# Two 32-column transposes in place of one 64-column transpose in a conditioned recurrent layer

## The chip, the cores and the metric

The kernel runs on one core of a Trainium2 chip. The core has five engines with instruction queues of their own: TensorE (PE in the profile; its weight loads are shown as PEld), VectorE (DVE), ScalarE (ACT), GpSimd (POOL) and SyncE (SP, which here only issues DMAs). The metric is the device time of one execution in microseconds.

## What is computed

```python
xT = jnp.swapaxes(x, 0, 1)
def step(h, x_t):
    fused = jax.nn.sigmoid(jnp.concatenate([x_t, h], axis=-1) @ w_W + w_b)
    hidden_state, output_state = jnp.split(fused, 2, axis=-1)
    memory_state = x_t @ wx_W + wx_b + hidden_state * (h @ wh_W + wh_b)
    h_new = output_state * h + (1.0 - output_state) * jnp.tanh(memory_state)
    return (h_new, h_new)
_, hs = jax.lax.scan(step, h0, xT)
return x + jnp.swapaxes(hs, 0, 1)
```

`x` is 8 x 512 x 512 (batch, time, features), the state `h` is 8 x 512, everything in float32. The loop of 512 steps is serial: each needs the `h` that the one before made. In the names of the kernel, `r` is `hidden_state`, `z` is `output_state`, and **hh** is `h @ wh_W + wh_b`.

## The kernel before

**Layout.** The 512 features of the state lie as 128 partitions x 4 chunks (k = 0 to 3) x 8 batches. Chunks 0 and 1 are half A (`hf = 0` in the code), chunks 2 and 3 are half B (`hf = 1`). One step of the loop over `i` (512 of them, written out, no loop on the chip) belongs to a group `g` of four steps; the buffers `md0`, `md1` and the PSUM banks alternate with `g % 2`.

**TensorE in a step** (L219, the helper `mm`). The order is A0 A1 A2 A3 D0 D1 D2 D3 H2 H3, the digit being the chunk of `h` that is the stationary operand: bank A receives 256 columns for chunks 0 and 1 and 192 for 2 and 3, bank D 128, bank H 64. Behind them come, in each step, some products of the input with its weights for a chunk of time 17 steps ahead (tiles `xp`); they depend on nothing in the step. A0 to A3 need the new state of their chunk, so A2 of the next step needs the new state of chunk 2, the first chunk of half B.

**VectorE in a step.** The order of its queue is the order in which the code is written (the schedule is manual). From the first wait on bank A:

1. `turn_r` L577 `tr<-A` transposes r of half A; `turn_h(0)` L592 `md1A<-A`; `turn_z` L577 `tz<-A` and the small memset `settle(0)` L600.
2. `memory(0, 0)` and `memory(0, 1)`: scans L565 `m<-md0A,md1A`, each followed on ScalarE by a tanh (L285 `hT<-m`).
3. `turn_part` L636 `md1B<-A`; `turn_r_b` L577 `tr<-D`, whose results ScalarE turns into `md0B` with one sigmoid for each chunk (L285 `md0B<-tr`), and into `sz` with one more.
4. `update(0, 0)` (L565 `hT<-hd0A,hT`, new state of chunk 0); **`turn_h(1)` L592 `md1B<-H`**, which transposes hh of half B, 128x64 in PSUM bank H, into slot 1 of `md1B` for both chunks of the half; `update(0, 1)`; **`settle(1)` L600**, a memset of one column that waits for `h_done[1]`, the completion of that transpose.
5. `memory(1, 0)` and `memory(1, 1)`: scans L565 `m<-md0B,md1B` of chunk 2 and chunk 3, each followed by its tanh.
6. `turn_sz` L629 `hd0B<-sz`: two transposes of 128x32, then a memset L632 that waits for the first of the two; `update(1, 0)` and `update(1, 1)` (L565 `hT<-hd0B,hT`), the new state of chunks 2 and 3.
7. Sums of the input products (L431), turns of the input parts (L319) and two memsets (L710) fill the time until bank A of the next step is complete.

**Waits.** An instruction here waits for a semaphore in its own queue, and all behind it wait too. VectorE also waits for itself: a scan that reads what a VectorE instruction shortly before it has written needs a wait for that write. One instruction carries one wait; a second one costs an instruction of the queue's own (EVENT_SEMAPHORE, engine DVEq in the trace). The memsets L600 and L632 carry such waits in place of it. ScalarE's tanh needs its scan, `update` needs its tanh and the transposed `z`.

**Names of the change.** `md1[hf][g % 2]` is seen as partition x 32 rows x 2 chunks x slots; in memory the chunk is the outer one. `raw["h"][1]` is `ps["H"]`, 64 columns, 32 for each chunk. `h_done` is set by `turn_h` and read by `settle`.

Of the kernel before, what the change touches and what calls it, by code (L numbers as in the profile page):

```python
# [76 lines left out]
def tile_cond_rnn_residual(  # L77
# [38 lines left out]
    nc = tc.nc  # L116
# [54 lines left out]
    def pair(n, name, rows, slots):  # L171

        return const.tile([P, 2, rows, slots], F32, name=name).rearrange("p c n s -> p n c s")
# [3 lines left out]
    NH = 2 * GS  # L177
# [4 lines left out]
    md1 = [[pair(n, f"md1{n}{i}", 32, m) for i in range(2)] for n, m in (("A", 2), ("B", 3))]  # L182
# [340 lines left out]
    pool_done = {}  # L523
    for i in range(T):
        g, s = divmod(i, GS)
        c, t = divmod(i, TC)
# [46 lines left out]
        raw = {"h": (pa[:, :HU], ps["H"]), "z": (pa[:, HU : 2 * HU],), "r": (pa[:, 2 * HU :], ps["D"][:, HU:])}  # L573
# [6 lines left out]
        h_done = [None, None]  # L580
# [8 lines left out]
            )  # L589

        def turn_h(hf):
            inst = nc.vector.transpose(  # L592
                md1[hf][g % 2][:, :, :, hf].rearrange("p n c -> p c n"), raw["h"][hf]
            ).ins
            h_done[hf] = inst
            if hf == 0 and i + 1 - NH in pool_done:
                tc.add_manual_dep(inst, pool_done[i + 1 - NH].name, SYNC)

        def settle(hf):
# [53 lines left out]

        turn_r()
        turn_h(0)
        turn_z()
        memory(0, 0)
# [6 lines left out]
        sz = turn_r_b()  # L664
        update(0, 0)
        turn_h(1)
        update(0, 1)
        settle(1)
# [146 lines left out]
```

## Time and profile before

| | |
|---|---|
| median of 3 runs | 1628.59 us (1627.81 to 1628.85) |
| span of the profiled execution | 1625.9 us |
| PE busy | 1616.3 us, 99% of the span |
| DVE busy | 1411.1 us, 87% |
| ACT busy | 1023.8 us, 63% |
| POOL busy | 539.1 us, 33% |
| granted TensorE clock | 1.000 |

The span runs from the first to the last instruction of the profiled execution; the median of the runs lies 2.7 us above it, which is what surrounds the instructions (the profiled execution has no other time of its own). Starts in a timeline are printed to 10 ns. A matmul's start is recorded and its end modelled. In a row of groups, the numbers after the bar are total busy time, mean duration in ns, and the idle time of the engine before the group with what ended it.

### The profile page before, as it was taken

Reading aid. Unit: us, or ns where it says so; the run is one execution under the profiler, and the core shown is the slowest. Engines: PE = TensorE matmul, PEld = TensorE weight load, DVE = VectorE, ACT = ScalarE, POOL = GpSimd, SP = SyncE. Lnnn points to the kernel's source line nnn. Section 1 sums busy time; section 2 is a strip of 40 time slices with the busy share of each in tenths; the row PEclk is TensorE's granted clock in tenths of the full one; section 3 lists DMA queues with packets and bytes.
Section 4 is the critical chain, followed back from the end, with each engine's and each line's share of the span. In section 5 each row is a group of like instructions: output and inputs, shape, how many; then the busy total and the mean of one; then the engine's idle time right before and its main releaser. Section 6 shows DMA issues by size and latency. Waiting matters only on the chain.

```text
span 1625.9 us, 120027 instructions
## 1 busy us (share of the span) xinstructions
PE 1616.3 (99%) x49211; PEld 1308.3 (80%) x49211; DVE 1411.1 (87%) x11757; ACT 1023.8 (63%) x6033; POOL 539.1 (33%) x1443
## 2 busy tenths in 40 slices
PE   9999999999999999999999999999999999999998
PEld 5888888888888888888888888888888888888876
DVE  8988888888888888888888888888888888888887
ACT  4666666666666666666666666666666666666665
POOL 2323333333333333333333333333333333333321
PEclk9999999999999999999999999999999999999999
DMA  4011111111111111111111111111111111110110
GB/s 192 12 40 33 29 37 38 43 32 33 31 43 39 35 34 31 39 38 39 33 29 37 38 43 32 30 35 43 38 33 34 32 39 38 39 34 25 31 35 10
DMA packets 66217, 62.04 MB, mean 38 GB/s; under 512 B 9856, under 2 KB 64000, under 8 KB 65664
## 3 DMA queue, kind: packets, MB, share of 16 engines
q1 hardware_dynamic: 65664, 54.35, 12.7%
q8 instruction: 385, 6.31, 1.7%
q14 instruction: 168, 1.38, 0.3%
HBM read 14.96 MB, written 8.39 MB: 14 GB/s over the span
## 4 chain that ended last, share of the span: by engine, by line
PE 98%; DVE 1%; issue 0%; ACT 0%; DVEq 0%
PE A L219 49%; PE D L219 27%; PE xp L219 16%; PE H L219 7%; DVE tr L577 0%; DVE m L565 0%; DVE md1B L636 0%; DVE hT L565 0%; DVE md1A L592 0%; DVE tz L577 0%; DVE zeros L185 0%; DVE hd0B L629 0%; DVE md1B L592 0%; DVE idle L600 0%; ACT hT L285 0%
## 5 line engine op out<-in xcount | busy, mean ns | idle before, releaser
L219 PE MATMUL A<-wa,hT 128*32 128x256 f32 x16352 | 877.8, 355 | 4.2 <-DVE hT L565 4.2
L219 PEld LDWEIGHTS A<-wa,hT 128*32 128x32 f32 x16352 | 497.5, 123 | 260.2 <-DVE hT L565 135.6
L219 PE MATMUL D<-wd,hT 128*32 128x128 f32 x16384 | 541.0, 273 | 0.0
L219 PEld LDWEIGHTS D<-wd,hT 128*32 128x32 f32 x16384 | 480.4, 122 | 21.8 <-DMA wd<-in_wd_dram 0.5
L731 POOL TENSOR_TENSOR ot<-xin,hT 128x32 f32<-128x32 f32 x503 | 134.4, 267 | 1046.5 <-DVE hT L565 1028.8
L285 ACT ACTIVATE md0A<-tr 128x16 f32<-128x16 f32 x512 | 112.9, 221 | 385.2 <-DVE tr L577 385.2
L285 ACT ACTIVATE hT<-m 128x8 f32<-128x8 f32 x2048 | 324.2, 207 | 46.8 <-DVE m L565 0.4
L577 DVE STREAM_TRANSPOSE tr<-A 128x64 f32<-128x64 f32 x511 | 127.8, 250 | 199.4 <-PE A L219 198.2
L285 ACT ACTIVATE hT<-hT 128x16 f32<-128x16 f32 x1024 | 232.3, 227 | 91.4 <-DVE hT L565 89.9
L219 PE MATMUL H<-wa,hT 128*32 128x64 f32 x8208 | 208.3, 219 | 0.0
L285 ACT ACTIVATE md0B<-tr 128x8 f32<-128x8 f32 x1024 | 160.0, 206 | 42.6 <-DVE tr L577 1.2
L219 PEld LDWEIGHTS H<-wa,hT 128*32 128x32 f32 x8208 | 185.6, 122 | 0.0
L565 DVE TENSOR_TENSOR_SCAN hT<-hd0B,hT 128x24 f32<-128x24 f32 x1024 | 171.4, 208 | 0.8 <-DVE hT L565 0.8
L565 DVE TENSOR_TENSOR_SCAN hT<-hd0A,hT 128x24 f32<-128x24 f32 x1024 | 171.9, 168 | 0.0
L565 DVE TENSOR_TENSOR_SCAN m<-md0B,md1B 128x24 f32<-128x24 f32 x1024 | 154.5, 193 | 0.5 <-issue 0.4
L629 DVE STREAM_TRANSPOSE hd0B<-sz 128x32 f32<-128x32 f32 x1024 | 148.5, 190 | 0.0
L565 DVE TENSOR_TENSOR_SCAN m<-md0A,md1A 128x16 f32<-128x16 f32 x1024 | 142.5, 181 | 5.1
L219 PE MATMUL xp<-ti,si 128*32 128x192 f32 (+1 forms) x3120 | 146.7, 295 | 0.0
L450 POOL TENSOR_TENSOR xs<-ff 128x192 f32<-128x192 f32 x240 | 139.5, 597 | 0.1
L636 DVE STREAM_TRANSPOSE md1B<-A 128x64 f32<-128x64 f32 x511 | 130.1, 255 | 0.0
L285 ACT ACTIVATE hd0A<-tz 128x16 f32<-128x16 f32 x512 | 116.6, 228 | 21.2
L592 DVE STREAM_TRANSPOSE md1B<-H 128x64 f32<-128x64 f32 x512 | 128.3, 251 | 0.0
(110 smaller groups left out, 1861.0 us busy)
## 6 DMA issues: line engine op xcount, KB each, us to landing
ff<-tt SPq DMA_DIRECT2D x120, 96.0 KB, 2.6
ff<-tt SPq DMA_DIRECT2D x120, 72.0 KB, 2.2
out_dram<-ot SPq DMA_DIRECT2D x128, 64.0 KB, 1.8
xin<-in_x_dram SPq DMA_DIRECT2D x112, 64.0 KB, 2.1
ff<-ff SPq DMA_DIRECT2D x60, 96.0 KB, 2.1
ff<-ff SPq DMA_DIRECT2D x60, 72.0 KB, 2.7
wx<-in_wx_dram SPq DMA_DIRECT2D x4, 768.0 KB, 7.3
wa<-in_wa_dram SPq DMA_DIRECT2D x4, 512.0 KB, 11.1
```

Source lines behind the costliest of these rows:

```text
L219: nc.tensor.matmul(out_, lhsT, rhs, start=start, stop=False, skip_group_check=True)
L285: inst = nc.scalar.activation(out_, in_, func, **kw).ins
L450: nc.gpsimd.tensor_tensor(to, a, b, ALU.add)
L565: return nc.vector.tensor_tensor_scan(*[t_[:, :, c_].rearrange("p n c s -> p (n c s)") for t_ in (out_, d0, d1)], 0.0, ALU.mult, ALU.add,).ins
L577: inst = nc.vector.transpose(t_.rearrange("p c n -> p (c n)"), raw[n][hf]).ins
L592: inst = nc.vector.transpose(md1[hf][g % 2][:, :, :, hf].rearrange("p n c -> p c n"), raw["h"][hf]).ins
L629: nc.vector.transpose(hd0[1][i % 2][:, :, q, 2], sz[:, 32 * q : 32 * q + 32]).ins
L636: nc.vector.transpose(md1[1][g % 2][:, :, :, 0].rearrange("p n c -> p c n"), ps["A"][:, :HU])
L731: pool_done[i + 1] = nc.gpsimd.tensor_tensor(ot[:, t], x_of(c, slice(0, NQ), t, 1), hTs[(i + 1) % NH][:, :, :, B * s1 : B * s1 + B, 2].rea ...
```

## The change

```diff
         def turn_h(hf):
+            if hf:
+                for q in range(2):
+                    at = slice(32 * q, 32 * q + 32)
+                    inst = nc.vector.transpose(md1[1][g % 2][:, :, q, 1], raw["h"][1][:, at]).ins
+                    h_done[1] = h_done[1] or inst
+                return
             inst = nc.vector.transpose(
-                md1[hf][g % 2][:, :, :, hf].rearrange("p n c -> p c n"), raw["h"][hf]
+                md1[0][g % 2][:, :, :, 0].rearrange("p n c -> p c n"), raw["h"][0]
             ).ins
-            h_done[hf] = inst
-            if hf == 0 and i + 1 - NH in pool_done:
+            h_done[0] = inst
+            if i + 1 - NH in pool_done:
                 tc.add_manual_dep(inst, pool_done[i + 1 - NH].name, SYNC)
```

For half B, the transpose of 64 columns becomes two of 32 columns, chunk 2 first, at the same place of the queue. `h_done[1]` keeps the first of them, so that `settle(1)` waits for chunk 2 alone. Half A is as before.

## Prediction

> **What bounds the kernel now.** I read the chain of waits first, cut to one ordinary step in the middle.
>
> ```profile
> 9 pieces in order of time: start us, us, what
> ...
> 802.97 1.54 PE A L219 x32
> 804.51 0.87 PE D L219 x32
> 805.38 0.22 PE H L219 x16
> 805.60 0.49 PE xp L219 x16
> 806.10 1.02 PE A L219 x17
> ```
>
> The chain is TensorE alone, and a step lasts 806.10 − 802.97 = 3.13 us. But the four pieces don't run at one pace. D has 32 matmuls of 128 columns, H 16 of 64, xp here 8 of 192 and 8 of 96: 7,424 columns in 0.87 + 0.22 + 0.49 = 1.58 us, 0.2128 ns a column. At this pace A's 16 x 256 + 16 x 192 = 7,168 columns need 1.525 us, and take 1.54. Some 15 ns are lost in A. The groups, shapes kept apart, and the table of waits tell where:
>
> ```profile
> L219 PE MATMUL A<-wa,hT 128*32 128x192 f32 x8176 | 435.5, 331 | 0.3 <-DVE hT L565 0.3
> L219 PE MATMUL xp<-ti,si 128*32 128x192 f32 x1920 | 122.0, 326 | 0.0
> ...
> PEld A L219 <- DVE hT L565: 135.6, 499, 0.8
> ```
>
> A matmul of 192 columns in A lasts 5 ns longer than the same shape in xp; there are 16 in a step, four at a time, so 5 x 16 / 4 = 20 ns of wall time. The weight loads wait 135.6 / 499 = 0.27 us a step for a scan `hT`. Most of that hides behind the matmuls of chunk 1; the 15 to 20 ns are what sticks out. The timeline shows which scan:
>
> ```profile
> 803.63 0.51 PEld L219 LDWEIGHTS A<-wa,hT 128*32 128x32 f32 x16 [0.27 <-DVE hT L565]
> ...
> 803.37 0.21 DVE L565 TENSOR_TENSOR_SCAN hT<-hd0B,hT 128x24 f32<-128x24 f32 x1
> 803.50 0.21 DVE L565 TENSOR_TENSOR_SCAN hT<-hd0B,hT 128x24 f32<-128x24 f32 x1
> ```
>
> The load for A2 comes 0.05 us after the end (803.58) of `update(1, 0)`. So TensorE is nearly at its own pace, and what exceeds it is a **loop**: A2, A3, end of bank A, VectorE's chain, `update(1, 0)`, A2. What makes `update(1, 0)` earlier gains at most 20 ns a step, 511 x 20 = 10.2 us; what makes it later is paid in full.
>
> VectorE's queue in this step:
>
> ```profile
> 801.63 0.21 DVE L592 STREAM_TRANSPOSE md1A<-A 128x64 f32<-128x64 f32 x1
> 801.76 0.21 DVE L577 STREAM_TRANSPOSE tz<-A 128x64 f32<-128x64 f32 x1
> ...
> 802.50 0.17 DVE L565 TENSOR_TENSOR_SCAN hT<-hd0A,hT 128x24 f32<-128x24 f32 x1
> 802.59 0.26 DVE L592 STREAM_TRANSPOSE md1B<-H 128x64 f32<-128x64 f32 x1
> 802.74 0.17 DVE L565 TENSOR_TENSOR_SCAN hT<-hd0A,hT 128x24 f32<-128x24 f32 x1
> 802.89 0.20 DVE L565 TENSOR_TENSOR_SCAN m<-md0B,md1B 128x24 f32<-128x24 f32 x1
> 802.91 0.06 DVE L600 MEMSET idle<- 128x1 f32 x1
> 803.01 0.18 DVE L565 TENSOR_TENSOR_SCAN m<-md0B,md1B 128x24 f32<-128x24 f32 x1
> 803.11 0.20 DVE L629 STREAM_TRANSPOSE hd0B<-sz 128x32 f32<-128x32 f32 x1
> 803.21 0.18 DVE L629 STREAM_TRANSPOSE hd0B<-sz 128x32 f32<-128x32 f32 x1
> 803.37 0.06 DVE L632 MEMSET idle<- 128x1 f32 x1
> ```
>
> Instructions overlap: the queue's cost of one is the distance to the next start, its duration is longer. The transpose of hh ends at 802.59 + 0.26 = 802.85, and the memset that waits for it stands at 802.91, 0.06 to 0.07 later. The same distance stands between the first sz transpose (end 803.31) and its memset (803.37): that is what a wait of VectorE for itself lasts. The chunk-2 scan ends at 803.09; an unheld scan lasts 0.17 (the two updates above), so it really got going at 802.92, just behind the memset. **The memset holds it**: the scan before, at 802.74, left the queue free at about 802.83 (a scan costs 0.09, from 802.50 to 802.59).
>
> **The change, part by part.**
>
> *The wait.* A 32-column transpose as first behind a scan lasts 0.20, so the first half would end at 802.79 and free the memset at 802.86. That wait then binds nothing, because the queue gets there later, as follows.
>
> *The second instruction.* No row shows a 32-column transpose out of PSUM. The nearest rows are the sz pair, 0.10 to 0.11 from start to start, and ends at 803.31 and 803.39, so 0.08 to 0.09 for the second. If the second costs between that and the first, a pair is 0.19 to 0.22, against 0.15 for the single one now (802.59 to 802.74): **0.04 to 0.07 more**. Bounds: nothing, if the cost went by columns alone; and 0.13, if the second costs what a 64-column transpose out of PSUM costs behind another (801.63 to 801.76). Columns alone are excluded by the sums:
>
> ```profile
> L431 DVE TENSOR_TENSOR ff<-xp,ee 128x384 f32<-128x384 f32 x60 | 31.9, 532 | 0.0
> L431 DVE TENSOR_TENSOR ff<-xp,ee 128x288 f32<-128x288 f32 x60 | 25.9, 432 | 0.0
> ```
>
> 96 columns more are 0.10 more, 1.04 ns each, so 64 columns are 0.067 of the 0.13 and some 0.06 is fixed; a half out of PSUM would then cost 0.06 + 0.033 = 0.10, which agrees with the sz pair. I take 0.06 for the addition.
>
> *The queue.* `update(0, 1)` goes from 802.74 to 802.80 and leaves the queue at 802.89 (0.09) to 802.90 (0.10, from 803.01 to 803.11). An unheld memset costs 0.01, as two of them in an early step without idle time show:
>
> ```profile
> 56.36 0.42 DVE L338 TENSOR_TENSOR ti<-wx,ti 128x192 f32<-128x192 f32 x1
> 56.72 0.24 DVE L577 STREAM_TRANSPOSE tr<-A 128x64 f32<-128x64 f32 x1
> 56.73 0.07 DVE L710 MEMSET idle<- 128x1 f32 x2
> ...
> 803.63 0.56 DVE L431 TENSOR_TENSOR tt<-xp,ee 128x384 f32<-128x384 f32 x1
> 804.11 0.20 DVE L319 STREAM_TRANSPOSE md1A<-xs 128x32 f32<-128x32 f32 x1
> ```
>
> With no memset between, the next start comes 0.08 before the end (804.11 against 804.19); with two, 0.06 before it (56.72 against 56.78), so 0.02 for both. The chunk-2 scan starts at 802.90 to 802.91 in place of 802.92, and with the addition at 0.04 or 0.07, anywhere from 802.88 to 802.92. The gain is 0.00 to 0.04; **I take 0.014**. ScalarE's sigmoid for the chunk is not in the way: it starts at 802.61 and lasts 0.21, so ends at 802.82.
>
> ```profile
> 802.61 0.31 ACT L285 ACTIVATE md0B<-tr 128x8 f32<-128x8 f32 x2
> 803.12 0.32 ACT L285 ACTIVATE hT<-m 128x8 f32<-128x8 f32 x2
> ```
>
> *Chunk 0 and 1 of the state.* `update(0, 0)` stands ahead of the change. `update(0, 1)` is 0.06 later and ends at 802.97. Its reader is A1:
>
> ```profile
> 802.79 1.72 PE L219 MATMUL A<-wa,hT 128*32 128x256 f32 x32
> ```
>
> A0 starts at 802.79 and is 8 matmuls of 256 columns, 0.44 us at 0.2128 ns, so A1 is due at 803.23; with 0.05 from scan to load it is in time by 0.2 us. No cost; without this cover it would be 0.06 a step, 31 us.
>
> *An own wait for the chunk-3 scan.* Today `memory(1, 1)` is covered by the memset's wait. The second half is not, so the scan needs a wait on VectorE beside the one on ScalarE, as `update(1, 1)` has for the second sz transpose:
>
> ```profile
> L565 DVEq EVENT_SEMAPHORE  x515: 21/21/21, 21.9 to 1623.0; - x172
> ```
>
> 515 of them, about one a step; I expect one more in each. `update(1, 1)` ends 0.13 behind `update(1, 0)` (803.71, 803.58), the chunk-3 scan 0.10 behind chunk 2's (803.19, 803.09): 0.03 for it. Behind it stand `turn_sz`, its memset and both updates of half B. `update(1, 0)` has two conditions: the tanh (starts at 803.12, lasts 0.21, ends 803.33 to 803.34) and the memset at 803.37. From memset to scan end the other place took 0.18 (802.91 to 803.09), which would give 803.55, while it ends at 803.58; so this branch has 0.03 to spare. It moves by 0.03 − 0.014 = +0.016, the tanh branch by −0.014: 803.566 on both. It costs nothing more, but nothing is left; if the slack weren't there, it would take 0.016 of the gain and turn it into nothing. The Trainium skill ("VectorE: DVE Perf Modes", § The DRAIN you can't avoid) says that a same-engine read after write isn't safe without a semaphore, which makes this wait likelier, and that in its measurement the semaphore cost nothing extra; by the latter the chunk-3 scan would gain as much as chunk 2's, and the sum would be the same. The trace's 0.03 speaks against nothing extra here.
>
> *Load.* VectorE has 0.06 + 0.03 more a step and today idles before bank A in nearly every step:
>
> ```profile
> DVE tr L577 <- PE A L219: 198.2, 491, 0.9
> ```
>
> 198.2 / 491 = 0.40 us a step hide it; in the 20 early steps without this wait it may cost 20 x 0.09 = 1.8 us at most; I take 0.3, since part of the wait removed comes off there too.
>
> **The sum**, against the profiled span: 511 x 0.014 = 7.2 us less, 0.3 more, so 1625.9 − 6.9 = 1619.0, and with the 2.7 around it about **1621.7 us**. The median of the runs shown is the span plus these 2.7.
>
> **Rivals.**
>
> *Given back.* If both halves cost 0.11, the scan starts at 802.92 as today, or the own wait takes the gain: 1628.6, within 3 us. For it: the gain is the small difference of a wait removed (0.07 to 0.09 of idle queue) and 0.04 to 0.07 of work put there. Against it: the second sz transpose's end, 0.08 behind the first.
>
> *Slower: the second transpose out of PSUM is dear.* The scan is no earlier from an addition of 802.92 − 0.01 − 0.09 − 802.74 = 0.08 on. At 0.13 it is 0.05 late, 511 x 0.05 = 26 us: **1654**. Halfway, 0.105, it is 1641. For it: every 64-column transpose out of PSUM in the table costs 0.13 or more, none of 32 is there. Against it: the fixed share of 0.06 worked out above. The Trainium skill ("Perfetto Trace Analysis", § Optimizing Scalar/DVE Operations) gives DVE about 60 ns for each instruction on SBUF and about 125 on PSUM, and advises larger operations. By it, as an estimate, the addition would be 0.125 and the time about 1652. The trace doesn't bear that out: 0.13 for 64 columns leaves no room for 0.125 of fixed cost beside 0.067 of columns.
>
> *It doesn't do what it says.* If the chunk-2 scan were made to wait for the second half as well (tracked by whole tile), that ends near 802.59 + 0.10 + 0.18 = 802.87, the wait is over at 802.94, 0.03 later than now: 1628.6 + 15 = 1644. Against it: the sz pair, where `update(1, 0)` goes at 803.37 without waiting for the second transpose (its end 803.39 + 0.07 = 803.46).
>
> **How the numbers follow.** This kernel's runs tell a change of 0.2%, 3.3 us or 6.4 ns a step, from none. Forecast (gain of 7 to 20 ns, 1618 to 1625): 0.50. Given back: 0.20. Dear second transpose: 0.20. Not what it says: 0.08. Something else: 0.02, half of it faster. Faster 0.51, same 0.20, slower 0.29. The likeliest case alone is 1618 to 1625.3. The low end is the full stall, 1628.6 − 10.2 = 1618.4, a little lower for its rounding; the high end reaches into the slower cases to 1641, the halfway price: below it lie the first two cases and half of the dear one, about 0.80.
>
> **What would show it.** In the profile after: 1024 transposes `md1B<-H` of 128x32, with starts 0.10 to 0.11 apart; `update(0, 1)` 0.20 to 0.22 behind the first; the memset no longer 0.07 behind a transpose's end; about 1,024 EVENT_SEMAPHOREs at L565; the mean of A's 192-column matmuls from 331 toward 326 and A in the chain toward 1.525. Wrong if the first half and `update(0, 1)` stand 0.24 or more apart, if the memset L632 moves later against bank A's end, or if the 192-column mean rises.

## The result and the profile after

The changed kernel takes 1636.03 us (median of 5 runs, 1635.33 to 1636.61) against 1628.59 (1627.81 to 1628.85): **0.46% slower**, ratio 1.0046, 95% interval 1.0034 to 1.0058. Run once more, beside the last experiments, it took 1634.06 against 1626.98 there (1.0045, 1.0031 to 1.0058). A gain of 7 us was forecast; the loss is 7 us.

The head of the page after, and its two rows of code on the way to the core. By their number the packets of `q8` hold TensorE's instructions (49211 + 49211 in 385 packets are 256 in each), those of `q14` the instructions of all other engines. `q14` had 168 packets and 1.38 MB before, `q8` the same as after.

```profile
span 1634.2 us, 121051 instructions
...
PE 1624.0 (99%) x49211; PEld 1309.0 (80%) x49211; DVE 1421.8 (87%) x12269; ACT 1025.9 (63%) x6033; POOL 538.9 (33%) x1443
...
q8 instruction: 385, 6.31, 1.6%
q14 instruction: 176, 1.44, 0.3%
```

VectorE's instructions rose from 11757 to 12269, by 512, the whole program's from 120027 to 121051, by 1024. The other 512 are the own waits, one a step, as foreseen. The 1024, all of VectorE, came in 8 more packets of `q14`, so **128 instructions of VectorE lie in one packet**. That will matter below.

The groups, shapes kept apart, the row of the own waits, and the table of waits, in the kernel after:

```profile
L219 PE MATMUL A<-wa,hT 128*32 128x192 f32 x8176 | 439.4, 332 | 0.8
```

```profile
L565 DVEq EVENT_SEMAPHORE  x1027: 21/21/21, 22.5 to 1631.3; - x172
```

```profile
DVE tr L577 <- PE A L219: 193.1, 492, 0.8
...
PEld A L219 <- DVE hT L565: 143.5, 502, 0.6
```

The 192-column matmuls of A went from 331 to 332 ns, not toward 326; the weight loads wait 143.5 us for the scans in place of 135.6. So `update(1, 0)` is later, not earlier. VectorE's queue in an ordinary step:

```profile
794.38 0.17 DVE L565 TENSOR_TENSOR_SCAN hT<-hd0A,hT 128x24 f32<-128x24 f32 x1
794.47 0.30 DVE L595 STREAM_TRANSPOSE md1B<-H 128x32 f32<-128x32 f32 x2
794.68 0.17 DVE L565 TENSOR_TENSOR_SCAN hT<-hd0A,hT 128x24 f32<-128x24 f32 x1
794.77 0.20 DVE L565 TENSOR_TENSOR_SCAN m<-md0B,md1B 128x24 f32<-128x24 f32 x1
794.80 0.06 DVE L606 MEMSET idle<- 128x1 f32 x1
794.89 0.19 DVE L565 TENSOR_TENSOR_SCAN m<-md0B,md1B 128x24 f32<-128x24 f32 x1
795.00 0.29 DVE L635 STREAM_TRANSPOSE hd0B<-sz 128x32 f32<-128x32 f32 x2
```

From the pair's start to `update(0, 1)` it is 0.21 (794.47 to 794.68), the price foreseen (0.20 to 0.22). The first half is over by 794.47 + 0.20 = 794.67 and its wait by 794.74, so nothing holds the memset at 794.80 any more. Yet the chunk-2 scan ends at 794.97, 0.50 behind the pair's start, just as it ended 0.50 behind the single transpose (802.59 to 803.09).

Rows of 10 ns can't show a few nanoseconds, so I took the recorded starts and ends of all ordinary steps (not the first and the last 16) of each traced kernel. Medians in ns, counted from the start of the transpose of r (`tr<-A`), and the step from one such start to the next; "late" is explained below; "time" is the median less that of the kernel before, run beside it:

```
                     upd(0,1)  chunk-2   chunk-3   upd(1,0)   step   late   time us
                     start     scan end  scan end  end
before               1282      1631      1729      2121       3118     9       -
changed              1346      1638      1746      2129       3126    19     +7.4
changed, again       1345      1637      1745      2127       3124    19     +7.1
e1 cover second      1345      1637      1778      2144       3140     8    +11.9
e2 own wait only     1281      1629      1755      2120       3117    19     +4.9
e3 two memsets       1345      1646      1745      2135       3131    23    +10.7
e4 no hold           1280      1611      1711      2101       3100     9     -6.9
e5 blocks apart      1344      1637      1746      2128       3126     0    +10.3
e6 blocks upon       1344      1637      1745      2129       3128   121    +56.7
e7 no memset         1344      1647      1749      2138       3137     0    +13.6
e8 before, apart     1275      1623      1722      2113       3162     0    +29.1
e9 pair aside        1345      1637      1735      2126       3123     9     +3.4
e10 pair aside bare  1345      1611      1711      2102       3100     9     -6.9
```

The ordinary step grew by 8 ns, which is 4 us in 511 steps. The rest sits elsewhere. Against the steps of the kernel before, 35 steps differ by more than 40 ns and sum to 4.7 us; the others are 7 ns longer at the median, 3.3 us together; the first of these steps starts 0.4 later. That makes 8.4, the difference of the spans being 8.3.

One of the 35, in the timeline of the changed kernel:

```profile
407.80 0.16 DVE L565 TENSOR_TENSOR_SCAN hT<-hd0A,hT 128x24 f32<-128x24 f32 x1
407.89 0.20 DVE L565 TENSOR_TENSOR_SCAN m<-md0B,md1B 128x24 f32<-128x24 f32 x1
407.92 0.06 DVE L606 MEMSET idle<- 128x1 f32 x1
408.35 0.21 DVE L565 TENSOR_TENSOR_SCAN m<-md0B,md1B 128x24 f32<-128x24 f32 x1 [0.26 <-ACT hT L285]
408.48 0.29 DVE L635 STREAM_TRANSPOSE hd0B<-sz 128x32 f32<-128x32 f32 x2
```

The chunk-3 scan starts 0.46 behind the chunk-2 scan in place of 0.12. The view names ScalarE as releaser, but `hT` of ScalarE is what comes behind this scan, and the sigmoid that the scan does need had ended at 407.93; nothing was late. The cause shows when VectorE's instructions are counted through, own waits included. These are the numbers of the instructions behind which the next one started more than 0.15 us later than usual (steps' ends and sums left aside):

```
changed:        574 1854 1982 2878 3134 3262 4158 4414 5438 5694 6718 6974 7998 9534 10558 10814 11838 12094
changed, again: the same
before:         62 830 1214 2494 4542 5822 7486 9150 10430 12094
remainder by 128: 62 in every case
```

(The column "late" above counts from the first step on and has one more of the changed kernel, ahead of a sum.)

They sit at the seams of the 128-instruction packets, and, of some 105 seams, at those that fall right behind a wait instruction (late by 0.35), or one or two instructions later (0.26, 0.19); three later it is about 0.10. Of the 18 of the changed kernel, 11 stand behind the new wait of the chunk-3 scan (4 times this scan is late, 7 times a transpose of sz), 5 at `update(1, 1)`, which had its own wait before, and 2 at waits of the sums. In the kernel before, three of the few cases are `update(1, 1)` itself, and most of the others are sums and turns behind it, where idle time follows.

### The profile page after: what moved, and what is told of

It reads as the page before. It is cut to its first block, busy times and chain, and to the rows that moved or that the text cites. A ratio compares the mean times of both kernels' runs of the same rounds, so it can differ in the third digit from the quotient of the medians.

```text
span 1634.2 us, 121051 instructions
## 1 busy us (share of the span) xinstructions
PE 1624.0 (99%) x49211; PEld 1309.0 (80%) x49211; DVE 1421.8 (87%) x12269; ACT 1025.9 (63%) x6033; POOL 538.9 (33%) x1443
## 4 chain that ended last, share of the span: by engine, by line
PE 97%; DVE 2%; issue 0%; ACT 0%; DVEq 0%
PE A L219 48%; PE D L219 26%; PE xp L219 15%; PE H L219 7%; DVE tr L577 1%; DVE m L565 1%; DVE hT L565 0%; DVE md1B L642 0%; DVE md1A L598 0%; DVE tz L577 0%; DVE hd0B L635 0%; ACT hT L285 0%; DVE md1B L595 0%; DVE zeros L185 0%; DVE idle L606 0%
## 5 line engine op out<-in xcount | busy, mean ns | idle before, releaser
L219 PEld LDWEIGHTS A<-wa,hT 128*32 128x32 f32 x16352 | 497.4, 123 | 267.9 <-DVE hT L565 143.5
L565 DVE TENSOR_TENSOR_SCAN hT<-hd0B,hT 128x24 f32<-128x24 f32 x1024 | 176.6, 208 | 1.9 <-DVE hT L565 1.4
L565 DVE TENSOR_TENSOR_SCAN m<-md0B,md1B 128x24 f32<-128x24 f32 x1024 | 159.2, 197 | 1.1 <-ACT hT L285 1.1
L595 DVE STREAM_TRANSPOSE md1B<-H 128x32 f32<-128x32 f32 x1024 | 153.9, 195 | 0.0
```

The costliest lines, as they stand in the source:

```text
L219: nc.tensor.matmul(out_, lhsT, rhs, start=start, stop=False, skip_group_check=True)
L565: return nc.vector.tensor_tensor_scan(*[t_[:, :, c_].rearrange("p n c s -> p (n c s)") for t_ in (out_, d0, d1)], 0.0, ALU.mult, ALU.add,).ins
L595: inst = nc.vector.transpose(md1[1][g % 2][:, :, q, 1], raw["h"][1][:, at]).ins
```

## The experiments

Theory W: the own wait that the change brings to the chunk-3 scan exposes the seams of VectorE's code, and that is half of the loss. Theory S and its rival M are about the other half: why the chunk-2 scan isn't earlier. The first four kernels ran on one chip, the next four on a second, the last three on a third, each beside the kernel before.

**e1: the second half's wait on a memset.**

```diff
+                    h_second[0] = inst
...
+        mark = nc.vector.memset(idle[:, IDLE - 1 : IDLE], 0.0).ins
+        tc.add_manual_dep(mark, h_second[0].name, SYNC)
         memory(1, 1)
```

> The changed kernel with one more memset, in front of the chunk-3 scan, that waits for the second transpose in place of the scan's own wait instruction. Theory W: VectorE's code comes in blocks of 128 instructions, and where a block begins at or up to three instructions behind a wait instruction of its queue, the next instruction is 0.1 to 0.35 us late; the changed kernel has 18 such lateness cases over 0.15 us and loses about 4 us by them. With the wait instructions gone from the chunk-3 scan, the cases behind it go (at most some 4 left, at the other wait instructions, which half of the time are hidden), the steady step stays about 7 ns longer than before: 1632 to 1633 us, wait instructions at L565 back to about 515. Rival R: the lateness has nothing to do with the wait instruction, all of the loss is the longer queue: 1636 or, with the memset's own cost, more.

1638.41 against 1626.54 us, ratio 1.0073 (1.0061 to 1.0086). The own waits and their late cases went, as W says:

```profile
L565 DVEq EVENT_SEMAPHORE  x515: 21/21/21, 22.2 to 1634.0; - x172
```

But the time forecast was missed. The chunk-3 scan ends 141 ns behind the chunk-2 scan in place of 108: the memset costs 0.03 more than the wait instruction did (43 ns more than the 98 of e9, which has neither), and now the branch through the sz transposes sets `update(1, 0)` (2144). The 0.03 us to spare there were used up.

**e2: the own wait alone, without the pair.**

```diff
-            scan(c_, ms[hf], md0[hf][g % 2][:, rows], md1[hf][g % 2][:, rows])
+            inst = scan(c_, ms[hf], md0[hf][g % 2][:, rows], md1[hf][g % 2][:, rows])
+            if hf and q:
+                tc.add_manual_dep(inst, late_update[0].name, SYNC)
...
-        update(0, 1)
+        late_update = [update(0, 1)]
```

> The kernel before, its 64-column transpose kept, with an own wait of VectorE added to the chunk-3 scan (for the update of chunk 1, which is long done). Theory W: the steady step stays as before (within 3 ns, since the branch through the chunk-3 scan has 0.03 us to spare), and some 15 to 25 late instructions of 0.2 to 0.35 us appear at block starts: 1631 to 1634 us. Rival R: no late instructions, 1628.6, or a steady loss of 0.02 us in every step, 1638.

1631.46 against 1626.54, ratio 1.0031 (1.0020 to 1.0042). The chunk-3 scan ends 26 ns later, `update(1, 0)` and the step are unchanged: the slack of 0.03 us was there. The late cases went from 9 to 19, on a kernel that differs in nothing else. The own wait costs 4.9 us though no ordinary step is longer.

The update of chunk 1 isn't long done, as was expected: it ends at 1445 here, the wait instruction starts 38 behind that, and the chunk-3 scan ends 311 behind it. The same holds in the changed kernel for what its own wait waits for, the second half: that ends at 1435, the wait instruction starts 39 later, and the scan ends 312 behind it. So both waits bind. The chunk-3 scan ends 126 behind the chunk-2 scan here and only 108 there (98 without such a wait, in the kernel before and in e9), because there what is awaited ends 10 ns earlier and the chunk-2 scan 9 ns later.

**e3: one memset more in front of the chunk-2 scan.**

```diff
         update(0, 1)
+        nc.vector.memset(idle[:, IDLE - 3 : IDLE - 2], 0.0)
         settle(1)
```

> The changed kernel with one more memset, without a wait, ahead of the one that waits for the first transpose. It tells what an unheld memset costs in front of the chunk-2 scan. Theory S (the scan lasts 0.20 us by itself, whether held or not, so that the memset held it for less than I had read): the scan ends 0.01 us later, 1641 us. Rival M (a memset costs 0.03 to 0.035 us here, not 0.01): the scan ends 0.03 later, 1651 us.

1637.24 against 1626.54, ratio 1.0065 (1.0051 to 1.0079). The scan ends 8 ns later than in the changed kernel. That spoke for S, though its time of 1641 was missed, and it misled: it priced a second memset, not the first (e10).

**e4: the hold taken away.**

```diff
+            to = aside[g % 2] if hf else md1[0][g % 2]
             inst = nc.vector.transpose(
-                md1[hf][g % 2][:, :, :, hf].rearrange("p n c -> p c n"), raw["h"][hf]
+                to[:, :, :, hf].rearrange("p n c -> p c n"), raw["h"][hf]
             ).ins
-            h_done[hf] = inst
+            h_done[hf] = h_done[hf] or inst
...
-        update(0, 0)
+        h_done[1] = update(0, 0)
         turn_h(1)
```

> The kernel before, with the 64-column transpose of hh of half B in its place but into a tile that nobody reads, and the memset waiting for the update of chunk 0; hh of half B is left out of the result. The chunk-2 scan then has no wait for the transpose, and no work is added. Theory: the chunk-2 scan ends 0.05 to 0.06 us earlier against the start of the transpose (the whole of what the wait held), the 192-column matmuls of A fall to 326 to 327 ns and the time to TensorE's own pace, 1618 to 1620 us. Rival: the memset held nothing, or the chain is set by another wait (the sigmoid, the sz transposes): within 3 us of 1628.6.

1619.60 against 1626.54, ratio 0.9957 (0.9944 to 0.9971). The step falls to 3100 and A's matmuls to TensorE's own pace:

```profile
L220 PE MATMUL A<-wa,hT 128*32 128x192 f32 x8176 | 428.2, 326 | 0.3 <-DVE hT L566 0.3
```

So the wait for the transpose was the right thing to aim at, and 7 us was all there was. But the scan's end moved by 20 ns only (1631 to 1611), not 50 to 60: right behind the wait stands the sigmoid of chunk 2, which ends 1372 behind the transpose of r and lets the scan start at 1404.

**e5 and e6: the seams moved.** Both pad the changed kernel to 512 instructions in 16 steps, so that the seams recur at fixed places of the step. They differ by 81 memsets at the start.

```diff
+    for _ in range(SHIFT):
+        nc.vector.memset(idle[:, :1], 0.0)
...
-        for n in range(IDLE - 3):
-            nc.vector.memset(idle[:, n : n + 1], 0.0)
+        more = (5 if i % 16 in (0, 8) else 6) if i >= 32 else 0
+        for n in range(IDLE - 3 + more):
+            nc.vector.memset(idle[:, n % 2 : n % 2 + 1], 0.0)
```

> The changed kernel with five or six idle memsets of one column more at the end of each step from step 32 on, in VectorE's idle time before bank A, and 32 at the start, so that 16 steps are 512 instructions, four blocks of 128, and every block begins at the same places of the step, none of them within four instructions behind a wait instruction of a scan. Theory W (a block that begins just behind a wait instruction is late by 0.1 to 0.35 us): no late instruction of over 0.15 us behind these waits after step 32, the steady step as in the changed kernel (3126 ns at the median), and the time 3 to 4 us above the kernel before, some 4 us below the changed kernel, though it has 2,800 instructions more. Rival R (late instructions come from something else, a DMA or a refresh, by time): as the changed kernel or a little more, 7.5 us above before.

> The same as the run before it, but with 113 memsets at the start in place of 32, which puts 120 block starts within four instructions behind a wait instruction, most of them directly behind. Theory W: about 120 late instructions, summing to 39 us; some of it is hidden where it is the chunk-3 update that is late: 25 to 39 us above the kernel with no block start there. Rival R: the same time as that kernel, within 2 us.

e5: 1637.93 against 1627.61, ratio 1.0063 (1.0049 to 1.0076); e6: 1684.33, ratio 1.0347 (1.0333 to 1.0361). No late case at a seam in e5, 121 in e6, which sum to 40 us; the spans are 1636.2 and 1681.5. Some 8 us of the difference arise before the padding of the steps begins: e6 starts step 32 at 131.3 us, e5 at 123.0, as the memsets at the start run to 31.3 us in place of 19.4. From step 32 to the end e6 takes 37.0 us more (1550.2 against 1513.2), for the same instructions, by where the code's seams fall: W is shown, and in its range of 25 to 39. The time of e5 was missed by 6 us, since the padding isn't free (e8). In e6 the loads of A wait far more:

```profile
PEld A L222 <- DVE hT L568: 199.6, 581, 6.5
```

**e7: the memset replaced by an own wait of the chunk-2 scan**, seams apart (padding as in e5, 35 at the start).

```diff
         update(0, 1)
-        settle(1)
```

> The changed kernel without the memset that waits for the first half, so that the chunk-2 scan waits by a wait instruction of its own, and with block starts put away from the wait instructions (two left within reach). Theory M1: a memset between two scans costs 0.02 to 0.03 us where nothing holds it, a wait instruction whose condition is already met less than 0.01; the chunk-2 scan then ends 0.01 us earlier than in the kernel before, the steady step is 3106 to 3112 ns, and the time 3 to 6 us below the kernel before. Rival S1: the scan lasts this long whatever stands ahead of it, or the wait instruction costs as much as the memset: steady step 3124 to 3128 ns, 3 to 4 us above before.

1641.20 against 1627.61, ratio 1.0084 (1.0070 to 1.0098). The chunk-2 scan ends at 1647, 10 ns later than with the memset. But the wait was not one already met, as M1 had it: its instruction starts 39 behind the end of the first half (1336), and the scan ends 311 behind that end, as in e2 and the changed kernel. So e7 prices a wait that binds, and neither forecast was put to the test; part of the time is the padding's.

**e8: the padding alone, on the kernel before** (512 instructions in 16 steps, 36 memsets at the start).

```diff
-        for n in range(IDLE - 3):
+        more = (7 if i % 16 in (0, 8) else 8) if i >= 32 else 0
+        for n in range(IDLE - 3 + more):
```

> The kernel before with seven or eight idle memsets more at the end of each step from step 32 on and 36 at the start, 512 instructions in 16 steps, no block start within reach of a wait instruction of a scan. It says what the padding does by itself. Theory W: the few late instructions of the kernel before (three on its path, about 0.45 us together) go, the steady step stays at 3118 ns: 0 to 1 us below the kernel before. If the padding did something else of its own, the step changes.

1656.74 against 1627.61, ratio 1.0179 (1.0165 to 1.0193). The expectation was wrong. A row of the timeline and one of the waits:

```profile
804.75 0.46 DVE L714 MEMSET idle<- 128x1 f32 x8
```

```profile
DVE tr L580 <- PE A L222: 10.2, 30, 0.6
```

Eight memsets take 0.46 us, not 0.09. The cause is in the edit: `n % 2` makes them write the same two columns in turn, and in the trace each from the third on carries a wait of VectorE for itself. Their starts are 8, 124, 24, 102, 25, 101 and 25 ns apart: each starts some 67 behind the end of the last that wrote its column, 71 and 90 at the first two. So the padding waits for itself. VectorE then waits for bank A in 30 steps in place of 491, and the padded tail sets the step. So e5, e7 and e8 show where late cases are, but their times hold the padding too; e5 against e6 from step 32 on is clean, as both have it.

**e9 and e10: the pair without its waits.** The pair writes a tile that nobody reads; in e10 so does the transpose of hh's first part (`turn_part`), and the memset is dropped. **e11** is the changed kernel, unedited, beside them.

```diff
+    aside = [pair(0, f"aside{i}", 32, 3) for i in range(2)]
...
-                    inst = nc.vector.transpose(md1[1][g % 2][:, :, q, 1], raw["h"][1][:, at]).ins
+                    inst = nc.vector.transpose(aside[g % 2][:, :, q, 1], raw["h"][1][:, at]).ins
...
-        update(0, 0)
+        h_done[1] = update(0, 0)
```

and, for e10 alone:

```diff
-            nc.vector.transpose(md1[1][g % 2][:, :, :, 0].rearrange("p n c -> p c n"), ps["A"][:, :HU])
+            nc.vector.transpose(aside[g % 2][:, :, :, 0].rearrange("p n c -> p c n"), ps["A"][:, :HU])
...
         update(0, 1)
-        settle(1)
```

> The changed kernel with both 32-column transposes in their place but into a tile that nobody reads, and the memset waiting for the update of chunk 0; hh of half B is left out of the result. The work of the pair stands in the queue, without any wait for it: no wait instruction at the chunk-3 scan. It splits the loss. Theory W with S: the chunk-2 scan ends where it does in the changed kernel (1638 ns behind the start of the transpose of r, within 3), the steady step is 3124 to 3127 ns, the late instructions at block starts are no more than 10, and the time is 3.5 to 4.5 us above before: half of the changed kernel's loss. Rival R (the pair alone makes the whole loss): 7 to 8 us above.

> The same without the memset, and with the transpose of hh's first part (line 636 before) into the unread tile as well, so that the chunk-2 scan stands directly behind the update of chunk 1 with neither memset nor wait instruction; this leaves that part out of the result too. Theory S (the scan lasts 0.20 us by itself): it ends 8 to 12 ns earlier than with the memset, at 1626 to 1630 ns, steady step 3114 to 3118. Rival M (a memset costs 0.02 to 0.03 us in front of a scan): it ends at 1608 to 1618 ns, with the sigmoid as its bound at 1611, steady step 3100 to 3106.

> The changed kernel once more, beside the two runs above on one chip. Theory W: steady step 3126 ns and 15 to 25 late instructions at block starts, at the same places of the instruction stream as in its first profile, since they are fixed by the program and not by time; 7 to 8 us above before, so some 4 us above the run with the pair into the unread tile.

e9: 1630.42 against 1626.98, ratio 1.0021 (1.0012 to 1.0031). e11, the changed kernel beside it: 1634.06. Of 7.1 us, **3.4 are the pair and its memset, 3.6 are the own wait of the chunk-3 scan**: the ordinary step is the same within 1 ns, and the late cases go from 9 to 19, with the same 18 as in the first profile.

e10: 1620.10, ratio 0.9956 (0.9943 to 0.9970). Its queue:

```profile
802.37 0.30 DVE L596 STREAM_TRANSPOSE aside<-H 128x32 f32<-128x32 f32 x2
802.58 0.16 DVE L566 TENSOR_TENSOR_SCAN hT<-hd0A,hT 128x24 f32<-128x24 f32 x1
802.66 0.28 DVE L566 TENSOR_TENSOR_SCAN m<-md0B,md1B 128x24 f32<-128x24 f32 x2
```

With neither memset nor own wait, the chunk-2 scan starts 0.08 behind `update(0, 1)` and ends at 1611, 26 ns earlier than with the memset (1637 in e9), the step at TensorE's pace. That end is set by the sigmoid, as in e4: it lies 239 behind the sigmoid's end, 240 in e4, within 3 ns in nine steps of ten, while against `update(0, 1)` it varies by 11. So the second transpose itself would have been free: it fits in front of the sigmoid's bound. M holds for the first memset behind a scan, which costs at least 0.026 with the wait that it carries, and e3's 0.008 was that of a second one directly behind it. S falls. Whether the memset costs this or its wait, met long before, no run separates.

## Why the prediction was wrong

**The bound** was right: a loop through `update(1, 0)` with 20 ns a step above TensorE's pace. e4 and e10 reach that pace and gain 6.9 us; 10.2 was the limit stated.

**The wait and the pair** were right. The first half's wait binds nothing (the scan ends at 1637 in e9 too, where the memset doesn't wait for it), and the pair costs 64 ns more (1346 against 1282), 60 taken.

**The step that failed is the queue's**, the one that turned these into a gain of 0.014 us. From the start of `update(0, 1)` to the end of the chunk-2 scan it counted 0.09 to 0.10 for the update, 0.01 for an unheld memset, from two memsets behind a sum, and 0.17 for the scan, the duration of the updates: 0.275 in all. It is 0.292 in the changed kernel (1346 to 1638) and in e9. Without the memset it is at most 0.266 (1345 to 1611 in e10), so the memset with its wait costs at least 0.026 in place of 0.01, which is nearly the whole miss of 0.017. The prediction's terms make 1282 + 60 + 275 = 1617, a gain of 14; the measured ones 1282 + 64 + 292 = 1638, a loss of 7. What the wait had held was not 0.074 us (60 + 14) but 0.057 (1631 less 1282 + 292), less than the 0.064 that the pair adds. The rival "given back" named this balance, with the pair at its dear end; the balance came out 7 ns past zero, with the pair near the price taken and the memset behind it underpriced.

**The own wait** was foreseen in number and place, its slack of 0.03 us was there (e2), and so the step wasn't charged for it; the chunk-3 scan lost 10 ns by it, 0.03 was taken. What was missed is what it does to the code stream: 3.6 us, most of it at the seams. This cost was put at nothing, and no rival held it. The trace of before did show such cases: the list above was to be had by counting its late instructions.

**The rivals.** The second transpose isn't dear (0.098 from its start to the next instruction's, no 0.13), and the chunk-2 scan doesn't wait for the second half: in e9, where it reads neither half, it ends at the same 1637.

**The 2.7 us** around the span are too many: every run for which both are listed has 1.7 to 1.9 between span and time, and the profiled execution of before was among the quicker ones. The forecast isn't moved by it, since 1628.59 - 6.9 is 1621.7 as well.

**The range** held the time, by luck: its upper part was there for a dear second transpose, which didn't come. The chances were on the wrong side, 0.51 for faster and 0.29 for slower.

## What to carry to other kernels

A wait that holds an instruction hides the cost of what stands in the queue before it, the waiting memset's own cost too. When the wait is removed by adding work, price everything that then comes into the open by the row of that very instruction in that very neighbourhood, and look for the next bound behind the wait (here the sigmoid, 20 ns further). Splitting an instruction in two also makes a second completion to be waited for: count the own waits that the split adds, and where the code's seams fall on them. And padding is no neutral filler: look at what it writes, and whether it waits for itself.

## What the runs showed of the hardware

VectorE's code came in packets of 128 instructions (1024 more made 8 more packets). A seam cost nothing that shows at most places, but 0.35 us directly behind a wait instruction of the queue, and up to 0.26 and 0.19 one and two instructions later. The places are fixed by the program: the same 18 in two profiles. The Trainium skill ("Runtime: NRT & Kernel Launch", § Instruction fetch mechanics) calls the cost of crossing a block mostly hidden and puts a block at 256 instructions; the runs agree on the first away from wait instructions, and on the 256 for TensorE's code (98,422 instructions in 385 packets), but show 128 for VectorE's. Why the cover is missing behind a wait stays open; the runs show the places and the cost alone.

A one-column memset on VectorE has no one price: 0.008 us directly behind another one (e3), at least 0.026 between `update(0, 1)` and the chunk-2 scan (e9, e10), 0.043 between the scans of chunks 2 and 3 (e1). In the last two cases the memset carries a wait that is met by then.

A wait of VectorE for itself has two prices. With a wait instruction of its own, the scan ended 311 to 312 ns behind the end of the awaited instruction (changed kernel, e2, e7); with a memset to carry the wait, 246 behind it (kernel before, 1385 to 1631). So the wait instruction is dearer by 65 ns where the wait binds; the memset costs its 0.026 or more where it doesn't.
